# Reordered bank releases and relocated additions in the two-step q and V of layer 1

## The chip, the cores and the metric

The kernel runs on one core of one Trainium2 chip. The metric is device time in microseconds (us) of one execution. The engines are written as in the profile: PE is TensorE's matrix multiplication and PEld its weight loads, DVE is VectorE, ACT is ScalarE, POOL is GpSimd, SP is SyncE (here only a queue for transfers).

## The reference, cut to what matters

Two attention blocks over `x` of shape (8, 512, 32, 32), all in 32-bit floats: eight samples of 512 channels by 1024 positions. Layer 0 is an eight-headed attention with a group norm in front. Layer 1 has one head over all 512 channels:

```python
n = (x - mean) * rsqrt(var + EPS); n = n * gn_gamma + gn_beta      # one mean, one var per sample
q, k, v = wq @ nf + bq, wk @ nf + bk, wv @ nf + bv                 # 512 x 1024 each
attn = softmax(q.T @ k * c ** -0.5)
out = wo @ (v @ attn.T) + bo;  x = x + out
```

The kernel folds `wk` into `wq` and `wo` into `wv` before the loop, and takes the norm out of the products: `q` and `V` are made from the plain `x`, and what the norm would have added comes in as vectors (`norm.c` onto q, `norm.bias()` onto the output).

## The kernel before, in words

The loop over samples `b` runs `layer0` (64 units of layer-0 attention, then `middle`, which makes v, q and k of the next sample and projects), then `attention1` (layer 1). The order on PE, ACT and DVE is the order in which the program is written (`tc.manual_schedule(engines={PE, ACT, DVE})`); POOL and SP are ordered by the framework, close to the program. [...]

Products of 2 by 2 blocks are made in Winograd's form, seven products in place of eight (`A11·B11`, `A12·B21`, `S1·T1`, `S2·T2`, `S3·T3`, `S4·B22`, `A22·T4`, where S and T are sums of blocks). In layer 1 each of the seven is itself made in this form: the "two-step" product. q and V of samples 0 to 6 are made so by `seven_by_two_steps` (L679), called from `make_q_twice` (L1693) and `make_v_all` (L1774). It works on four groups of seven steps. Group z makes the inner products of outer products 1 and 4, w those of 5, c those of S1·T1 and A22·T4, and d those of A12·B21 and S4·B22, straight onto z. Each group has a bank of PSUM called `line` and one called `single`: `sz`/`oz`, `sw`/`ow`, `sc`/`oc`, `sd`/`od`. After each step a copy on ACT (L703) or an addition on DVE (L705) takes the bank's content to SBUF, and only then may a later step write that bank afresh. PSUM is handed out in tiles of two banks, two tiles of each tag, so c follows z in the same tiles, d follows w, and the next product's z and w follow c and d.

The first half alternates z and w, 14 steps. Then DVE makes four additions (L712 with q's bias, L710 without): `z1 += z0` for both k, `w += z1` for both k. The second half is c, c, d, c, d, c, d, ..., d, d. In its midst, after the last step of c, stand four more additions on DVE (L710): `z1 += c0` (128x512) and the long `c += w` (128x1024), for k = 1 and 0. The additions that empty the last two banks of d (`od`, `sd`) follow these in DVE's queue. After q, ACT adds the bias onto z (L736) and DVE makes `bias` (L400 to L402, three small operations). V then begins, and from step 0 on POOL makes q's sums S1 to S4 (`finish_q`, L1772, eight additions of 128x512) and the sums of S1's quarters (`halve_a`, L520, four of 128x256). After V come the scores (`line`, L1839, and `twice`, L1856), whose first banks are those of V's c and d.

The norm's averages are small matmuls (L305) into the unused second bank of z's `oz` tile (`room`, L288; `sample_average`, L302), read by DVE (L307): the mean after step 5, the variance after step 8.

`make_twice` (L583) sums the quarters of a weight for the second step and stores them in HBM; it is done once per weight. In sample 0 it runs for `v0`, `p0` and half of `wqk1` within the attention's units, on DVE, and for the other half of `wqk1` and half of `wvo1` in `middle`, on POOL, at steps 1 to 10 of v's product. Its loads and stores go through SP's queue, as does the gather of the softmax sums (`gather_couple`, L1325), on whose landing DVE's reciprocal (L1334) waits.

Of the kernel before, what the change touches and what calls it, by code (L numbers as in the profile page):

```python
# [65 lines left out]
def two_attention_blocks(  # L66
# [612 lines left out]
    def seven_by_two_steps(multiply, at, z, c, w, bias, name):  # L679

        def group(tag, products, use_of):
            line, single = (banks(t, f"ps_{t}{tag}_{name}") for t in "so")
            spares.append(single[:, 1, :])  # L690
            line, single = line[:, 0, :], single[:, 0, :]
            for bank, x, y, start, fresh, r, t in [
                (line, "A11", "B11", True, True, 0, 0), (single, "A12", "B21", True, False, 0, 0),
                (line, "S2", "T2", False, True, 0, 1), (single, "S1", "T1", True, True, 1, 1),
                (line, "S3", "T3", False, False, 1, 1), (single, "S4", "B22", False, False, 0, 1),
                (line, "A22", "T4", False, True, 1, 0),
            ]:
                multiply(bank, products, x, y, start)
                tiles, always = use_of
                to = at(tiles, r, t)  # L700
                of = bank[:, : len(products) * 2 * P].rearrange("p (i q) -> p i q", i=to.shape[1])
                if fresh and not always:
                    nc.scalar.copy(to, of)  # L703
                else:
                    nc.vector.tensor_tensor(to, of, to, ALU.add)  # L705
                yield

        def plus(to, x, y, by=None):
            if by is None:
                nc.vector.tensor_tensor(to, x, y, ALU.add)  # L710
            else:
                nc.vector.scalar_tensor_tensor(to, x, by, y, ALU.add, ALU.add)  # L712

        yield from together(group("z", REST[0], (z, False)), group("w", REST[1], (w, False)))
        for k in range(2):
            plus(z[k][:, 1, :], z[k][:, 0, :], z[k][:, 1, :], bias and bias(k, 0))
        for k in range(2):
            plus(w[k], w[k], z[k][:, 1, :], bias and bias(k, 1))
        one = group("c", [("S1", "T1"), ("A22", "T4")], (c, False))
        two = group("d", [("A12", "B21"), ("S4", "B22")], (z, True))  # L720
        spares.clear()
        next(one)
        yield
        n = 0
        for g in [one, two] * 6 + [two]:
            next(g)
            n += 1
            if n == 11:
                for k in [1, 0]:
                    plus(z[k][:, 1, :], z[k][:, 1, :], c[k][:, 0, :])  # L730
                    plus(c[k], c[k], w[k].unsqueeze(1).to_broadcast([P, 2, HALF]))
            if n < 13:
                yield
        if bias:
            for k in range(2):
                nc.scalar.activation(z[k][:, 0, :], z[k][:, 0, :], AF.Identity, bias=bias(k, 0))  # L736
        yield
        spares.clear()

# [407 lines left out]
    def layer0(bs, qs, ks, vs, b, norm_next, ending, begun):  # L1147
# [69 lines left out]
        if b == 0:  # L1217
            w = next_weight("qk13")
            w.finish()
            p0 = waiting[-1]  # L1220

            def bias0():
                rows = Rows([(bias_0, p0.moving)], 1, "bias0", room("bias0"))
                rows.store()
                rows.fetch(nc.sync)
                throughs[:] = [rows]

            hooks = {
                4: [lambda: norm_next.mean_of_all()], 5: [lambda: norm_next.variance_of_all()],
                **{6 + half: [lambda half=half: norm_next.normed(norm_next.xs, [half])] for half in range(2)},  # L1230
                8: [bias0, lambda: combine.first(norm_next.xs), lambda: score(0)],
                9: [combine.second, lambda: score(1), lambda: make_all("qk13", rows_of=both_of(w))],
            }
            hooks[7].append(p0.finish)
            at_steps(together(*pairs_qk(w, 1, bs, qs, ks, b)), hooks)
            for n, name in enumerate(["v0", "p0", "wqk1"]):
                of = [columns_of(of) for of in waiting if of.name == name]
                for i, step in enumerate(make_twice(name, rows_of=of[0] if of else None)):
                    at_units[8 + 12 * n + 2 * i - i // 3] = [step]
        else:  # L1240
            ps[0], = begun
            accs[units[0][:2]] = ps[0]
            score(1)
            if norm_next is not None:

# [249 lines left out]
    def middle(b, bs, twice_w, twice_b, comb, combine2, bias, hooks_v, divisions):  # L1495
# [3 lines left out]
        to, comb_twice, xs = {"qs": [None] * NC, "ks": [None] * NC}, {}, []  # L1499
        v_pairs = places_v(f"0_{b + 1}")  # L1500
        hooks_v.setdefault(8, []).append(lambda: twice_w.append(WeightTwice("qk02")))
        if b == 0:
            steps = [s for name in ["wqk1", "wvo1"] for s in make_twice(name, range(2, 4), None, nc.gpsimd)]
            for n, step in enumerate(steps):
                hooks_v.setdefault(1 + n, []).append(step)
        at_steps(
            make_v_twice(next_weight("v0"), twice_w.pop(0), bs, twice_b, v_pairs, f"v_0_{b + 1}"), hooks_v
        )
# [59 lines left out]
    def attention1(xs, norm, ready, b, at_values, norms):  # L1568
# [124 lines left out]
        def make_q_twice(w):  # L1693


            parts = ready.weights.all(columns_of(w))

            def multiply(bank, products, x, y, start):
                for i, (a, v) in enumerate(products):
                    nc.tensor.matmul(  # L1700
                        bank[:, i * 2 * P : (i + 1) * 2 * P], parts[a][x], twice_b[v][y],
                        start=start and i == 0, stop=True, skip_group_check=True,
                    )

            def at(tiles, r, t):
                cols = slice(t * 2 * P, (t + 1) * 2 * P)
                return tiles[r][:, :, cols] if len(tiles[r].shape) == 3 else tiles[r][:, cols].unsqueeze(1)

            z, c = ([tile2(f"{n}_q_1_{b}_{r}") for r in range(2)] for n in "zc")
            u = halves(tile2(f"w_q_1_{b}"))  # L1710

            def bias(k, i):
                return norm.c_up[:, k : k + 1] if i else norm.c[:, k : k + 1]

            of["A11"], of["A21"] = ([z[k][:, i, :] for k in range(2)] for i in range(2))
            of["A22"], of["A12"] = ([c[k][:, i, :] for k in range(2)] for i in range(2))
            return seven_by_two_steps(multiply, at, z, c, u, bias, f"q_1_{b}")

        of, hooks_v = {}, {}
        if last:  # L1720
            hooks = {
                1: [lambda: ready.measure(1), lambda: combine.make(1), lambda: combine.make(2)],
# [11 lines left out]
            (of["A11"], of["A21"]), (of["A12"], of["A22"]) = ([halves(t) for t in ts] for ts in qs)  # L1734
        else:
            hooks = {
                1: [norm.both_halves], 5: [norm.mean_of_all], 8: [norm.deviation], 12: [norm.untaken],
                16: [lambda: twice_w.append(WeightTwice("wvo1"))],
            }
            if b + 2 < B:  # L1740
# [9 lines left out]
                def measure_later(n):  # L1750
                    norms[b + 2].moments(n // 2, n % 2, n % 2 == 0)

                hooks[0], hooks[10] = ([lambda i=i: load_later(i)] for i in range(2))
                for n in range(4):
                    hooks.setdefault(15 + 3 * n, []).append(lambda n=n: measure_later(n))
                    hooks_v.setdefault(15 + 3 * n, []).append(lambda n=n: measure_later(n + 4))
                hooks_v[26] = [lambda: norms[b + 2].both_halves()]
                at_values[5] = [lambda: norms[b + 2].mean_of_all()]
                at_values[7] = [lambda: norms[b + 2].deviation()]
            at_steps(make_q_twice(w), hooks)  # L1760
        bias = norm.bias()

        w = next_weight("wvo1")

# [36 lines left out]
        if last:  # L1801
            v_pairs = places_v(f"1_{b}")
            for n in range(1, 5):
                hooks_v.setdefault(2 * n + 3, []).append(lambda n=n: finish_q(n, nc.vector))
            hooks_v[17] = [lambda: halve_a("S1")]
            at_steps(make_v_twice(w, twice_w[0], bs, twice_b, v_pairs, f"v_1_{b}"), hooks_v)
            v_of.update({(n, i): [t[:, i, :] for t in v_pairs[n]] for n in range(2) for i in range(2)})
        else:
            for n in range(1, 5):
                hooks_v.setdefault(0, []).append(lambda n=n: finish_q(n, nc.gpsimd))  # L1810
            hooks_v[0].append(lambda: halve_a("S1", None, nc.gpsimd))
            at_steps(make_v_all(w), hooks_v)


# [888 lines left out]
```

## Time and profile before

| | |
|---|---|
| three runs | 2852.02 us median (2847.18 to 2854.32) |
| the profiled execution | 2853.48 us, its span 2851.7 us |
| mean granted PE clock | 0.991 |
| PE busy | 2790.8 us, 98% of the span |
| DVE busy | 2185.8 us, 77% |
| ACT busy | 1193.4 us, 42% |
| POOL busy | 674.6 us, 24% |

The span runs from the first to the last instruction of one execution. Busy is the time in which at least one instruction of an engine runs[...]. PE's ends are modelled: a matmul of 256 columns has a record of 0.59 us for a pair while the next pair starts 0.43 us later, so a gap between products is some 0.17 us longer than the idle time that the profile writes beside it.

### The profile page before, as it was taken

How to read it: one execution, taken by the hardware profiler on the slowest of the kernel's cores; microseconds unless marked ns; L12 is line 12 of the kernel's file. 1: busy time of each engine (PE TensorE's matmuls, PEld its weight loads, DVE VectorE, ACT ScalarE, POOL GpSimd, SP SyncE). 2: the span in 40 equal slices, each digit the busy share in tenths (PEclk: the TensorE clock that was granted, in tenths of full speed). 3: DMA queues.
4: the chain of work that ended last, by engine and by line, in shares of the span. 5: the costliest groups of instructions: out<-in, count | busy, mean ns of one | idle time of the engine just before them, and what ended most of it. 6: DMA issues, size and time to landing. Idle time of an engine off the chain costs nothing. (4 is left out here: it accounts for less than half of the span.)

```text
span 2851.7 us, 42440 instructions
## 1 busy us (share of the span) xinstructions
PE 2790.8 (98%) x16570; PEld 1665.5 (58%) x16570; DVE 2185.8 (77%) x2997; ACT 1193.4 (42%) x1939; POOL 674.6 (24%) x706
## 2 busy tenths in 40 slices
PE   9998999999999999999999999999999999999999
PEld 5436674377643776437764477644776356763375
DVE  6786778876878768887778876787778877687877
ACT  3462443624346153462535524355342653226632
POOL 0003450015400254002530035300443005420021
PEclk9999999999999999999999999999999999999999
DMA  7535613255142551426423264322633236240101
GB/s 256 195 109 208 232 56 130 61 196 203 56 137 57 207 188 56 141 61 225 163 85 112 75 222 151 117 82 73 236 137 137 68 82 248 82 166 26 39 27 38
DMA packets 117552, 366.50 MB, mean 129 GB/s; under 512 B 25388, under 2 KB 26188, under 8 KB 110944
## 3 DMA queue, kind: packets, MB, share of 16 engines
q1 hardware_dynamic: 90576, 301.26, 30.7%
q10 hardware_dynamic: 26768, 62.46, 6.6%
q8 instruction: 132, 2.16, 0.3%
q14 instruction: 76, 0.62, 0.1%
HBM read 259.85 MB, written 79.99 MB: 119 GB/s over the span
## 5 line engine op out<-in xcount | busy, mean ns | idle before, releaser
L941 ACT ACTIVATE p<-s 128x1024 f32<-128x1024 f32 x505 | 516.5, 1024 | 308.5 <-PE s L1137 301.4
L943 DVE TENSOR_TENSOR acc<-acc,p 128x1024 f32<-128x1024 f32 x384 | 468.5, 1220 | 62.6 <-ACT p L941 53.9
L1137 PE MATMUL s<-qk_back,qk_back 64*64 64x512 f32 x3528 | 457.5, 590 | 0.0
L1186 PE MATMUL ps_o<-p,v_back 64*64 64x512 f32 x3528 | 455.4, 589 | 0.0
L1186 PEld LDWEIGHTS ps_o<-p,v_back 64*64 64x64 f32 x3528 | 135.0, 133 | 243.6 <-issue 240.0
L1137 PEld LDWEIGHTS s<-qk_back,qk_back 64*64 64x64 f32 x3528 | 132.6, 133 | 245.5 <-issue 216.4
L537 POOL TENSOR_TENSOR B_twice_p<-o 128x512 f32<-128x512 f32 x14 | 20.9, 1494 | 931.3 <-DVE o L1206 931.3
L2021 PE MATMUL ps_o<-t_p,s_v 128*128 128x512 f32 x384 | 169.6, 596 | 0.0
L1830 ACT ACTIVATE p<-p,factor 128x512 f32<-128x512 f32 (+1 forms) x112 | 84.6, 780 | 113.6 <-DVE p L1866 86.7
L2021 PEld LDWEIGHTS ps_o<-t_p,s_v 128*128 128x128 f32 x384 | 71.9, 190 | 88.4 <-issue 87.7
L1866 DVE TENSOR_TENSOR p<-ps_l,p 128x512 f32<-128x512 f32 x136 | 91.5, 687 | 40.3 <-PE ps_l L1856 38.3
L537 POOL TENSOR_TENSOR B_twice<-x 128x512 f32<-128x512 f32 x23 | 35.6, 1548 | 358.7 <-DVE x L1446 177.2
L1844 ACT COPY p<-ps_s 128x512 f32<-128x512 f32 x96 | 53.1, 588 | 134.4 <-PE ps_s L1839 134.4
L943 DVE TENSOR_TENSOR acc<-p,p 128x1024 f32<-128x1024 f32 x57 | 69.7, 1222 | 49.9 <-ACT p L941 49.9
L1035 PE MATMUL ps_l_qk<-t,w_qk 128*128 128x512 f32 x224 | 100.3, 595 | 0.3
L1866 DVE TENSOR_TENSOR p<-ps_s,p 128x512 f32<-128x512 f32 x112 | 74.8, 685 | 26.1 <-PE ps_s L1856 20.4
L641 ACT COPY c_q<-ps_s_qk 128x512 f32<-128x512 f32 x56 | 32.7, 583 | 140.0 <-PE ps_s_qk L1028 140.0
L1827 POOL TENSOR_TENSOR acc<-acc,p 128x512 f32<-128x512 f32 x48 | 83.6, 1741 | 13.3 <-ACT p L1830 10.8
L373 POOL TENSOR_TENSOR rstd<-rstd,minus_half 128x4 f32<-128x4 f32 (+1 forms) x16 | 12.9, 806 | 281.1 <-DVE rstd L372 281.1
L1035 PEld LDWEIGHTS ps_l_qk<-t,w_qk 128*128 128x128 f32 x224 | 42.0, 190 | 56.3 <-issue 50.2
L1839 PE MATMUL ps_s<-z_q,x 128*128 128x512 f32 x112 | 57.2, 636 | 14.1 <-DVE z_v L705 14.1
L659 DVE TENSOR_TENSOR c_v<-ps_l_v,c_v 128x512 f32<-128x512 f32 x64 | 42.6, 688 | 32.3 <-PE ps_l_v L784 32.2
(783 smaller groups left out, 6018.7 us busy)
## 6 DMA issues: line engine op xcount, KB each, us to landing
x<-in_x SPq DMA_DIRECT2D x64, 512.0 KB, 9.3
qk_back<-kept_qk SPq DMA_DIRECT2D x56, 512.0 KB, 6.3
w_qk<-stored_qk SPq DMA_DIRECT2D x14, 1792.0 KB, 8.5
fold<-acc SPq DMA_DIRECT2D x56, 256.0 KB, 3.1
qk_twice<-stored_qk_twice ACTq DMA_DIRECT2D x28, 512.0 KB, 3.9
kept_v<-c_v SPq DMA_DIRECT2D x28, 512.0 KB
kept_qk<-c_q SPq DMA_DIRECT2D x28, 512.0 KB, 3.3
kept_qk<-c_k SPq DMA_DIRECT2D x28, 512.0 KB, 3.5
```

The source lines that it names most:

```text
L537: engine.tensor_tensor(t[:, 0:4:2, :], part[:, :, 2 * P :], part[:, 0, :].rearrange("p (n q) -> p n q", n=2), ALU.subtract,)
L941: nc.scalar.activation(p, s, AF.Exp, scale=factor)
L943: nc.vector.tensor_tensor(acc, first, p, ALU.add)
L1035: nc.tensor.matmul(bank, of(i, a)[:, k, :], bs[v][:, k, :], start=start and k == 0, stop=k == 1, skip_group_check=True,)
L1137: nc.tensor.matmul(s[cols, j, :], ks[pair][k0 // HALF][rows, k0 % HALF : k0 % HALF + HD], qs[pair][g][rows, :], start=True, stop=True,)
L1186: nc.tensor.matmul(o[cols, half, :], vs[n][kt % 4 // 2][rows, h, c0 : c0 + HD], p[rows, j, :], start=kt == 0, stop=kt == NT - 1,)
L1827: engine.tensor_tensor(acc[:, i, :], acc[:, i, :], seen[i][-1], ALU.add)
L1830: nc.scalar.activation(p, p, AF.Exp, scale=norm.factor)
L1839: nc.tensor.matmul(bank, bs[v][:, k, t * P : (t + 1) * P], of[a][k], start=a == "A11" and k == 0, stop=k == 1, skip_group_check=True,)
L1844: nc.scalar.copy(to[:, t % 2, :], bank)
L1866: nc.vector.tensor_tensor(at(r, t), bank, at(r, t), ALU.add)
L2021: nc.tensor.matmul(bank, v_parts[kt // 2][a][:, kt % 2, c * P : (c + 1) * P], p_parts[kt // 2][b][:, kt % 2, cols], start=fresh and kt == ...
```

## The change

It has five parts. The first half's order becomes z, z, w, z, w, ..., w, w. In the second half, whose order stays, the additions of DVE come in another order: those that empty d's last two banks first, then `z1 += c0`; the long `c += w` go to POOL. ACT's bias onto z of q and POOL's `finish_q` and `halve_a` move from the end of q and step 0 of V to step 2 of V. `norm.bias()` and `both_halves` move into q's steps, the variance's average from step 8 to step 9, the measuring of sample b + 2 by ACT from steps 15, 18, 21, 24 to 14, 17, 19, 21. The weights' sums that POOL made in `middle` of sample 0 are made by DVE in the attention's units of sample 0, all steps from unit 3 on at a pitch of 1.5 units (before: from unit 8 on, at about 1.7 to 2).

```diff
-        yield from together(group("z", REST[0], (z, False)), group("w", REST[1], (w, False)))
+        def in_order(order, **groups):
+            for n in order:
+                next(groups[n])
+                yield
+
+        spares.clear()
+        first = dict(z=group("z", REST[0], (z, False)), w=group("w", REST[1], (w, False)))
+        yield from in_order("zzwzwzwzwzwzww", **first)
         for k in range(2):
             plus(z[k][:, 1, :], z[k][:, 0, :], z[k][:, 1, :], bias and bias(k, 0))
         for k in range(2):
             plus(w[k], w[k], z[k][:, 1, :], bias and bias(k, 1))
...
-        n = 0
-        for g in [one, two] * 6 + [two]:
-            next(g)
-            n += 1
-            if n == 11:
-                for k in [1, 0]:
-                    plus(z[k][:, 1, :], z[k][:, 1, :], c[k][:, 0, :])
-                    plus(c[k], c[k], w[k].unsqueeze(1).to_broadcast([P, 2, HALF]))
-            if n < 13:
-                yield
-        if bias:
-            for k in range(2):
-                nc.scalar.activation(z[k][:, 0, :], z[k][:, 0, :], AF.Identity, bias=bias(k, 0))
+        c_of, d_of = [("S1", "T1"), ("A22", "T4")], [("A12", "B21"), ("S4", "B22")]
+        second = dict(c=group("c", c_of, (c, False)), d=group("d", d_of, (z, True)))
+        yield from in_order("ccdcdcdcdcdcd", **second)
+        next(second["d"])
+        for k in [1, 0]:
+            plus(z[k][:, 1, :], z[k][:, 1, :], c[k][:, 0, :])
+        for k in range(2):
+            both = w[k].unsqueeze(1).to_broadcast([P, 2, HALF])
+            nc.gpsimd.tensor_tensor(c[k], c[k], both, ALU.add)
         yield
...
-            for n, name in enumerate(["v0", "p0", "wqk1"]):
+            steps = []
+            for name, ns in [("v0", range(2)), ("p0", range(2)), ("wqk1", range(4)), ("wvo1", range(2, 4))]:
                 of = [columns_of(of) for of in waiting if of.name == name]
-                for i, step in enumerate(make_twice(name, rows_of=of[0] if of else None)):
-                    at_units[8 + 12 * n + 2 * i - i // 3] = [step]
+                steps += make_twice(name, ns, of[0] if of else None)
+            for n, step in enumerate(steps):
+                at_units.setdefault(3 + 3 * n // 2, []).append(step)
...
-        if b == 0:
-            steps = [s for name in ["wqk1", "wvo1"] for s in make_twice(name, range(2, 4), None, nc.gpsimd)]
-            for n, step in enumerate(steps):
-                hooks_v.setdefault(1 + n, []).append(step)
...
+            def onto_first():
+                for k in range(2):
+                    nc.scalar.activation(z[k][:, 0, :], z[k][:, 0, :], AF.Identity, bias=bias(k, 0))
+
+            hooks_v[2] = [onto_first]
...
-                1: [norm.both_halves], 5: [norm.mean_of_all], 8: [norm.deviation], 12: [norm.untaken],
+                0: [norm.both_halves], 5: [norm.mean_of_all], 9: [norm.deviation],
+                12: [norm.untaken, lambda: biases.append(norm.bias())],
...
-                    hooks.setdefault(15 + 3 * n, []).append(lambda n=n: measure_later(n))
-                    hooks_v.setdefault(15 + 3 * n, []).append(lambda n=n: measure_later(n + 4))
+                    hooks.setdefault([14, 17, 19, 21][n], []).append(lambda n=n: measure_later(n))
+                    hooks_v.setdefault([14, 17, 19, 21][n], []).append(lambda n=n: measure_later(n + 4))
...
-        bias = norm.bias()
+        bias = biases[0] if biases else norm.bias()
...
-                hooks_v.setdefault(0, []).append(lambda n=n: finish_q(n, nc.gpsimd))
-            hooks_v[0].append(lambda: halve_a("S1", None, nc.gpsimd))
+                hooks_v[2].append(lambda n=n: finish_q(n, nc.gpsimd))
+            hooks_v[2].append(lambda: halve_a("S1", None, nc.gpsimd))
```

The last sample makes q and V by other functions (`make_q`, `make_v_twice`) and is not touched.

More of the change, by code (lines that the diff above doesn't have):

```diff
@@ L718, in seven_by_two_steps @@
             plus(w[k], w[k], z[k][:, 1, :], bias and bias(k, 1))
-        one = group("c", [("S1", "T1"), ("A22", "T4")], (c, False))
-        two = group("d", [("A12", "B21"), ("S4", "B22")], (z, True))
         spares.clear()
-        next(one)
-        yield
-        n = 0
-        for g in [one, two] * 6 + [two]:
-            next(g)
-            n += 1
-            if n == 11:
-                for k in [1, 0]:
-                    plus(z[k][:, 1, :], z[k][:, 1, :], c[k][:, 0, :])
-                    plus(c[k], c[k], w[k].unsqueeze(1).to_broadcast([P, 2, HALF]))
-            if n < 13:
-                yield
-        if bias:
-            for k in range(2):
-                nc.scalar.activation(z[k][:, 0, :], z[k][:, 0, :], AF.Identity, bias=bias(k, 0))
+        c_of, d_of = [("S1", "T1"), ("A22", "T4")], [("A12", "B21"), ("S4", "B22")]
[7 more added lines that the diff above has]
+            nc.gpsimd.tensor_tensor(c[k], c[k], both, ALU.add)
         yield
@@ L1717, in make_q_twice @@
             return seven_by_two_steps(multiply, at, z, c, u, bias, f"q_1_{b}")
-        of, hooks_v = {}, {}
+        of, hooks_v, biases = {}, {}, []
         if last:
@@ L1751, in measure_later @@
                     norms[b + 2].moments(n // 2, n % 2, n % 2 == 0)
-                hooks[0], hooks[10] = ([lambda i=i: load_later(i)] for i in range(2))
+                for i in range(2):
+                    hooks.setdefault(10 * i, []).append(lambda i=i: load_later(i))
                 for n in range(4):
-                    hooks.setdefault(15 + 3 * n, []).append(lambda n=n: measure_later(n))
-                    hooks_v.setdefault(15 + 3 * n, []).append(lambda n=n: measure_later(n + 4))
+                    hooks.setdefault([14, 17, 19, 21][n], []).append(lambda n=n: measure_later(n))
+                    hooks_v.setdefault([14, 17, 19, 21][n], []).append(lambda n=n: measure_later(n + 4))
                 hooks_v[26] = [lambda: norms[b + 2].both_halves()]
```

## The prediction

> **What bounds the kernel now.** I read the page first, then the granted clock, then PE's waits.
>
> ```profile
> span 2851.7 us, 42440 instructions
> PE 2790.8 (98%) x16570; PEld 1665.5 (58%) x16570; DVE 2185.8 (77%) x2997; ACT 1193.4 (42%) x1939; POOL 674.6 (24%) x706
> ```
> ```profile
> core 0: 2851.7 us, clock 0.991
> ```
> ```profile
> PE ps_sw_v L1782 <- DVE z_q L705: 21.7, 7, 3.1
> PE ps_s L1839 <- DVE z_v L705: 14.1, 7, 2.0
> PE ps_l_v L784 <- DVE c_v L659: 9.4, 1, 9.4
> PE ps_oz_q L1700 <- DVE mean_m L307: 1.8, 7, 0.3
> ```
>
> PE sets the end. It idles 2851.7 - 2790.8 = 61 us, and 0.009 of the clock costs another 26 us, so no reordering can win more than 87. Three waits for DVE hold 45 of the 61: the start of V (seven times), the start of the scores (seven times), and one long wait in sample 0. A table by stage, one stretch per sample from q's first product to the end of the scores' first block, says what these stages lose together (columns: stretch, us, then each engine's busy time, clock, DMA):
>
> ```profile
> 1719.73:1795.17 75.44, 69.34 (x359) 55.97 (x358) 47.77 (x76) 32.16 (x72) 34.14 (x48) 0.93 0.35 129
> 2071.02:2143.88 72.86, 65.76 (x359) 52.32 (x358) 50.29 (x76) 31.96 (x72) 35.55 (x48) 1.00 0.37 134
> sum 515.86, PE 472.14 PEld 380.53 DVE 343.60 ACT 212.32 POOL 240.97; mean PE 67.45 PEld 54.36 DVE 49.09 ACT 30.33 POOL 34.42
> ```
>
> The products alone, at the distance at which they follow each other undisturbed in the timeline (q 0.86 us, w's half as much; V 0.89 and 0.445; scores 1.72 and 0.86), need 21.1 (q) + 21.8 (V) + 19.8 (scores) + 0.3 (averages) = 63.0 us. Seven samples take 515.9, so 515.9 - 441 = **75 us** is lost. The timeline of sample 3 shows the cause: the long addition stands before the two that empty banks.
>
> ```profile
> 1394.77 1.22 DVE L710 TENSOR_TENSOR c_q<-c_q,w_q 128x1024 f32<-128x1024 f32 x1
> 1395.92 0.68 DVE L705 TENSOR_TENSOR z_q<-ps_od_q,z_q 128x512 f32<-128x512 f32 x1
> 1396.52 0.68 DVE L705 TENSOR_TENSOR z_q<-ps_sd_q,z_q 128x512 f32<-128x512 f32 x1
> 1397.25 0.71 PE L1782 MATMUL ps_sw_v<-w_wvo,t 128*128 128x128 f32 x4 [3.10 <-DVE z_q L705]
> ```
>
> [...] from 1397 to 1402 us the granted clock averages 0.66, and V's 128-column products follow at twice their distance. Laid on the trace's clock events, a window with 2.16 us of idle or more was followed by a slow one, one with 2.13 or less was not; each slow window costs 1.7 us of work. [...] in sample 5, where DVE's middle additions of V met POOL's 128x256 sums:
>
> ```profile
> 2108.34 1.85 POOL L520 TENSOR_TENSOR S_twice<-s_q 128x256 f32<-128x256 f32 x2
> 2108.76 1.98 DVE L710 TENSOR_TENSOR z_v<-z_v 128x512 f32<-128x512 f32 x2 [0.93 <-ACT z_v L703]
> 2110.67 2.35 DVE L710 TENSOR_TENSOR w_v<-w_v,z_v 128x512 f32<-128x512 f32 x2
> 2113.67 0.60 PE L1782 MATMUL ps_oc_v<-wvo_twice,T_twice 128*128 128x128 f32 x3 [0.16 <-DVE c_v L705]
> ```
>
> Undisturbed two of these take 1.28. Here they alternate strictly with POOL, 1.14 us for each pair, which is 0.68 + 0.73 less 0.27 of overlap. [...]
>
> **The change, part by part** (per sample of the seven; V starts at 0).
>
> *1. Banks first, end of q.* d's last addition now runs 0.2 to 0.9, and w's first step, third in the new order, wants the bank at 2 x 0.89 = 1.8. The 3.1 wait goes. *End of V:* the same; the second score line wants its bank at 1.72 + 0.86 = 2.6, free at 0.9. The 2.0 wait goes. The waits for ACT's copy of z7 (0.4 each, q and V) go too, as two steps of w now follow z7. ACT's moved bias (2 x 0.72) lies before the copy of z3, wanted three steps later: nothing. The measuring keeps its place in ACT's queue relative to the copies: nothing.
>
> *2. Long additions on POOL.* By the slope of POOL's rows (0.73 for 256 columns, 1.27 for 512) one of 1024 takes 2.4. They start when `z1 += c0` is done (2.2): 2.2 to 7.0. q's sums queue behind them: 8 x 1.23, to 16.9; S1's quarters, 4 x 0.68, to 19.6 (before: at 16.6 of V). The scores need those more than 26 us after V's start: hidden. But DVE's four middle additions of V come at 9.4, and POOL is now in its 128x512 sums until 17. A pair costs 0.68 + 1.27 - 0.27 = 1.68. First wait some 0.6, then 0.55 + 3 x 1.68: done at 15.6, c2's addition behind them at 16.3 to 16.4. The fourth step of c (its bank is c2's) is due at 9.3 + 5 x 0.89 = 13.8. **A new stall of 2.7** (1.9 to 3.1 by the first wait; 0.2 if DVE were let through). With 2.7 us, the chance that 2.16 of it lie in one window is (3.41 - 2.16 + 0.54) / 3.41 = 0.52, so 0.9 us of clock.
>
> *3. Long additions after V.* On POOL they meet DVE's sums of A12's quarters (four of 128x256) in the scores: DVE waits for two of 2.4, then alternates with S4's. The addition behind them ends near 9.1 after the scores begin, wanted at 9.5: nothing, bounds 0 and 2. POOL's later sums stand some 9 us later relative to PE than before; their first user comes 12 us after this block: nothing.
>
> *4. Averages.* The row `ps_oz_q <- mean_m` shows that the two banks of a tile are one to the waits. The mean now follows z4, which wrote that tile and must be copied first: 0.2 + 0.58 + 0.06 = 0.84. The variance follows z6 and its DVE addition: 0.2 + 0.69 + 0.06 = 0.95. Before, the wait lay behind the average: 0.42 and 0.46. *`norm.bias()` in q:* three small operations, 0.5, and the order's end put q's middle additions 1.3 to 1.7 later; c4 of q then waits 0.5 (0 to 0.9). Before, those three took 0.85, 1.2 and 1.18, blocked by POOL.
>
> Losses after: 0.84 + 0.95 + 0.5 + 2.7 + 0.9 = 5.9 per sample, 41 in seven, against 75. **Gain 34.**
>
> *5. Weights' sums of sample 0.* SP held the gather behind two stores that waited for POOL, DVE's reciprocal behind the gather, PE behind DVE:
>
> ```profile
> 245.09 2.08 SPq L611 DMA_DIRECT2D stored_wvo_twice<-wvo_twice  x2
> 247.27 0.59 SPq L1330 DMA_DIRECT2D few<-sums  x1
> 249.52 0.35 DVE L1334 RECIPROCAL few<-few 128x32 f32<-128x32 f32 x1 [10.53 <-DMA few<-sums]
> 251.06 1.22 PE L784 MATMUL ps_l_v<-w_v,t 128*128 128x256 f32 x2 [9.35 <-DVE c_v L659]
> ```
>
> 9.5 of stall go, and three slow windows (10.2 us at half clock), 5.1: 14.6. The other samples show no such wait, so none comes next. In the attention DVE gets six more sums of 4 x 0.24 us, 5.7, and five more loads, which land 3.1 to 4.5 us after issue where the first sum comes 1.8 to 3.6 later. DVE was idle 10.6 of the 80 us from 120 to 200, PE never: I take 1 us of cost, bounds 0 and 6. **Gain 13.6.**
>
> The sum: 2851.7 - 34 - 13.6 = 2804. The profiled execution was 1.8 longer than its span and 1.5 over the median: **2805**. A measurement of this kernel tells some 0.3% (8.6 us) from no change.
>
> **The rivals.** *B, DVE is let through* (or POOL's sums run elsewhere): part 2's stall and its clock vanish, 7 x 3.4 = 24: 2781. The strict alternation in sample 5 speaks against it; POOL's order is not the program's, which speaks for some of it. *C, the lock costs more*: the scores' addition is late by 2 each sample, the new V stall always trips the clock (0.8 more), the attention costs 6: 2805 + 20 + 5 = 2830. Part 3's margin of 0.4 us speaks for it. *D, slower*: a broadcast 128x1024 addition on POOL is far from linear. Beyond 2.6 us each, every us more in the two delays the scores' addition by two. At 6 us PE waits 6.8 there in each sample and loses two windows (3.4), with 1 of POOL's lateness elsewhere: 7 x 11 = 78: 2883. It ends slower from 4.9 us on (4.6 + 1.7 of clock, 7 x 6.3 = 44, and C's attention). POOL's rows at two widths lie on a line through 0.2, which speaks against it. *E*: the averages trip no clock, 0.84 and 0.95 being 2.6 us apart.
>
> **How the numbers follow.** A (the sum above) 0.62, its own range 2794 to 2818; B 0.18; C 0.13; D 0.05, a mishap that nothing shows 0.02. The range 2782 to 2831 takes in the ends of the unknown costs and most of B and C. Faster by over 0.3%: 0.91; within: 0.04; slower: 0.05.
>
> **What would show it.** Right: no rows `ps_sw_v <- z_q`, `ps_s <- z_v`, `ps_l_v <- c_v`; new rows of PE for `ps_oc_v <- DVE c_v` near 2.5 each and L305 behind `z_q` of ACT and DVE, 0.7 and 0.8 each; DVE's middle additions of V near 1.7 each; the seven stretches near 69 us. Wrong: a wait over 3 us in the scores, in V's first half or in the first attention; POOL's long additions over 3 us.

## The result, and the profile after

The changed kernel takes **2815.39 us** (median of 4 runs, 2814.06 to 2822.12) against 2852.23 for the kernel before (4 runs): a ratio of **0.9878, 95% interval 0.9858 to 0.9899**. The forecast was 2805 (2782 to 2831). The medians differ by 36.8 us, where 47 was forecast. The profiled execution took 2814.56 us, with a span of 2812.1, 39.6 less than before. The first lines of the page after, and the granted clock:

```profile
span 2812.1 us, 42413 instructions
PE 2771.6 (99%) x16570; PEld 1648.4 (59%) x16570; DVE 2197.6 (78%) x2993; ACT 1197.3 (43%) x1939; POOL 741.0 (26%) x710
```
```profile
core 0: 2812.1 us, clock 0.999
```

PE does the same 16570 matmuls in 19 us less busy time, as the clock rose from 0.991 to 0.999, and idles 41 us where it idled 61. PE's waits after (engine, tile, line, releaser; then us in total, times, longest):

```profile
PE ps_oc_v L1786 <- DVE c_v L705: 18.9, 7, 2.7
PE ps_oz_q L305 <- DVE z_q L705: 6.1, 7, 0.9
PE ps_oz_q L305 <- ACT z_q L703: 5.4, 7, 0.8
PE ps_sum L1315 <- DVE acc L1307: 2.3, 1, 2.3
```

The three waits that held 45 us are gone, each as forecast. Four new ones took their place. The first, at V's fourth step of c, is the new stall of the prediction's step 2 (2.7 there, 2.7 here). The next two are step 4's averages. The last, in the first attention, the prediction only had as part of a bound. The seven stretches from q's start to the end of the scores' first block say how evenly it goes (stretch, us, busy PE, PEld, DVE, ACT, POOL, granted clock, DMA share, GB/s):

```profile
1351.49:1420.45 68.96, 64.50 (x359) 52.06 (x358) 50.11 (x72) 32.56 (x72) 42.77 (x49) 1.00 0.39 141
2040.46:2110.80 70.34, 65.87 (x360) 53.42 (x358) 50.06 (x72) 32.56 (x72) 42.85 (x49) 0.98 0.38 139
sum 484.19, PE 452.91 PEld 365.81 DVE 350.84 ACT 216.39 POOL 297.95; mean PE 64.70 PEld 52.26 DVE 50.12 ACT 30.91 POOL 42.56
```

They took 515.86 before and 484.19 now: 31.7 us of the 39.6. Sample 5 alone met a slow window (3.41 us in which PE is granted half its clock) and is 1.4 longer. The rest of the gain, 7.6 us, is there when q of sample 0 starts (325.66 us before, 318.03 after).

The new stall in the timeline of V, sample 3 (start, us, engine, line, operation; V starts at 1375.68, lines of one engine are merged where they follow each other):

```profile
1384.92 2.95 POOL L1776 TENSOR_TENSOR s_q<-s_q,z_q 128x512 f32<-128x512 f32 x2
1385.15 3.27 DVE L710 TENSOR_TENSOR z_v<-z_v 128x512 f32<-128x512 f32 x2
...
1387.84 3.39 POOL L1776 TENSOR_TENSOR s_q<-z_q 128x512 f32<-128x512 f32 x2
1388.34 3.43 DVE L710 TENSOR_TENSOR w_v<-w_v,z_v 128x512 f32<-128x512 f32 x2
1391.70 0.68 DVE L705 TENSOR_TENSOR c_v<-ps_oc_v,c_v 128x512 f32<-128x512 f32 x1
1392.43 1.16 PE L1786 MATMUL ps_oc_v<-wvo_twice,T_twice 128*128 128x128 f32 x8 [2.70 <-DVE c_v L705]
```

DVE's four middle additions need 6.6 us, 1.65 each (1.68 forecast, 0.64 undisturbed), one for each of POOL's sums beside them (1.70 for each of the two at 1387.84, 1.27 for the one at 1383.69). The addition that empties the bank stands behind them, and PE behind that. Which of POOL's works made this, and what each part of the change is worth, is what the experiments ask.

### The profile page after: what moved, and what is told of

It reads as the page before. It is cut to its first block, busy times and chain, and to the rows that moved or that the text cites. A ratio compares the mean times of both kernels' runs of the same rounds, so it can differ in the third digit from the quotient of the medians.

```text
span 2812.1 us, 42413 instructions
## 1 busy us (share of the span) xinstructions
PE 2771.6 (99%) x16570; PEld 1648.4 (59%) x16570; DVE 2197.6 (78%) x2993; ACT 1197.3 (43%) x1939; POOL 741.0 (26%) x710
## 3 DMA queue, kind: packets, MB, share of 16 engines
q8 instruction: 132, 2.16, 0.3%
## 4 chain that ended last, share of the span: by engine, by line
PE 93%; DVE 3%; issue 2%; DMA 1%; ACT 0%; ACTq 0%; SPq 0%; POOL 0%; DVEq 0%; POOLq 0%
PE ps_o L1185 15%; PE s L1136 14%; PE ps_o L2025 10%; PE ps_l L1860 5%; PE ps_l_qk L1034 5%; PE ps_s L1843 4%; PE ps_s L1860 4%; PE ps_s_qk L1027 3%; PE ps_l_v L783 3%; PE ps_l_p L768 3%; PE ps_o_qk L1027 2%; PE ps_s_v L1055 2%; PE ps_s_p L1092 2%; PE ps_s_two L2155 2%; PE ps_o_v L1055 2%
## 5 line engine op out<-in xcount | busy, mean ns | idle before, releaser
L661 DVE SCALAR_TENSOR_TENSOR c_q<-ps_l_qk,vec,c_q 128x512 f32<-128x512 f32 x56 | 40.8, 749 | 34.2 <-PE ps_l_qk L1034 33.8
L659 DVE TENSOR_TENSOR c_v<-ps_l_v,c_v 128x512 f32<-128x512 f32 x64 | 42.7, 689 | 31.3 <-PE ps_l_v L783 31.2
```

## The experiments

The theory: PE's new stall comes from POOL's sums of q meeting DVE's middle additions, and the gain comes from DVE being free at V's start. The rivals: the order of the additions alone pays; POOL's long additions cause the stall; the new order of z and w frees the banks. No run takes part 3 (POOL's sums and ACT's bias from step 2 on) or the early `norm.bias()` by itself. Each ratio below is to the kernel before on the same chip, with its 95% interval.

### POOL's sums held back (e1_gate)

```diff
-            for n in range(1, 5):
-                hooks_v[2].append(lambda n=n: finish_q(n, nc.gpsimd))
-            hooks_v[2].append(lambda: halve_a("S1", None, nc.gpsimd))
+            hooks_v[2].append(lambda: finish_q(1, nc.gpsimd))
+            for n in range(2, 5):
+                hooks_v.setdefault(14, []).append(lambda n=n: finish_q(n, nc.gpsimd))
+            hooks_v[14].append(lambda: halve_a("S1", None, nc.gpsimd))
...
             of[f"S{n}"] = halves(tile2(f"s{n}_q_{b}"))
+            if n == 2 and u_of:
+                part = of["S2"][0][:, :NC]
+                engine.tensor_tensor(part, u_of[1][:, :NC], u_of[1][:, :NC], ALU.add)
...
             u = halves(tile2(f"w_v_1_{b}"))
+            u_of.extend(u)
```

> In V of samples 0 to 6, POOL's sums S2 to S4 of q now wait until DVE's four middle additions are done (a 4-column POOL instruction ahead of S2 reads what the last of them wrote). Theory, POOL's 128x512 sums and DVE's middle additions exclude each other: each middle addition takes 0.65 to 0.7 us in place of 1.63 to 1.75, PE's wait for c_v falls from 2.7 to 0.2 us in each sample, the one slow clock window of sample 5 goes too: 7 x 2.5 + 1.4 = 19 less, about 2796 us. Rival, the additions are late for another reason (ACT's copies, or a wait shifted to the scores, whose sums S now come up to 3 us later): the wait stays at 2.7 or as much comes back in the scores, 2815 us.

**2791.06 us, ratio 0.9792 (0.9778 to 0.9805)**, 24.3 less than the changed kernel. The wait for `c_v` is not in the list any more. The timeline of V's middle in sample 3 of this kernel:

```profile
1374.61 2.19 DVE L710 TENSOR_TENSOR z_v<-z_v 128x512 f32<-128x512 f32 x2
1376.73 1.28 DVE L710 TENSOR_TENSOR w_v<-w_v,z_v 128x512 f32<-128x512 f32 x2
1377.93 0.68 DVE L705 TENSOR_TENSOR c_v<-ps_oc_v,c_v 128x512 f32<-128x512 f32 x1
1378.09 0.20 POOL L1773 TENSOR_TENSOR s_q<-w_v 128x4 f32<-128x4 f32 x1 [2.43 <-DVE w_v L710]
```

DVE waits once for the sum that POOL is still in (2.19 for two), then runs free (1.28 for two), and POOL's next sum starts behind it. V's second half falls from 15.52 to 12.55 us. So the stall was these sums, and nothing came back in the scores (19.78 us against 19.89). It is the prediction's rival B made by hand, priced there at 24 less. More was gained than the 19 expected of the run: a wait of 2.7 cost 2.97 of PE's time (15.52 less 12.55), and the slow window in the first attention did not fall here (q of sample 0 starts 1.3 earlier).

### The long additions on DVE (e3_dvelong), and the order alone (e11_order)

```diff
-            nc.gpsimd.tensor_tensor(c[k], c[k], both, ALU.add)
+            nc.vector.tensor_tensor(c[k], c[k], both, ALU.add)
```

> The long additions c += w (128x1024) run on DVE behind the two additions z1 += c0, not on POOL, nothing else. Theory, their move to POOL pays by leaving DVE free at V's start: DVE is 2.5 us later there, the bank oz of V is freed at 5.4 us in place of 2.9 and PE waits 1.5 to 2.0 in V's first half; POOL starts q's sums 2.2 us earlier, so the middle additions meet fewer of them and the wait for c_v falls from 2.7 to 1.5 or 2.5; in the scores nothing: 7 x (+0.8 to +1.5), about 2823 us (2815 to 2832). Rival, POOL's long additions are what pushes its sums into the middle additions, and without them the wait for c_v is gone: below 2808 us.

**2836.92 us, ratio 0.9950 (0.9936 to 0.9963)**: 21.5 slower than the changed kernel, against 8 expected. PE's waits in it:

```profile
PE ps_oc_v L1786 <- DVE c_v L705: 12.9, 7, 1.9
PE ps_oz_v L1786 <- DVE z_v L705: 11.2, 7, 1.6
PE ps_s L1860 <- DVE p L1870: 11.2, 7, 1.6
```

The first two are as expected. The third was not: with the long additions of V on DVE, the addition in the scores comes 1.6 late. There the prediction's step 3 had given POOL's version a margin of 0.4 us, and DVE's has none. Three more slow windows in V (four, where the changed kernel has one) took some 5 us of the 21.5. The rival falls as the whole cause: without the long additions on POOL the middle additions still wait, though the stall is 1.9 where it was 2.7.

The other half of the question, in the kernel before:

```diff
-            if n == 11:
+            if n == 13:
```

> The kernel before with one number changed: the four additions of DVE in the second half (z1 += c0, c += w) come after the two that empty d's last banks, all still on DVE; no other part of the change. From e3_dvelong (2836.9 with the long additions on DVE, against 2839.0 for part 5 alone): the order alone only shifts PE's waits, V's start (3.1) and the scores' start (2.0) go, and in their place come the bank oz of V (about 1.6), the scores' addition onto p (1.6) and c_v in V's middle (1.9): 2850 us, within 8. Rival, the order is the part that pays, as the prediction's step 1 has it (3.1 + 2.0 a sample and fewer slow windows): 2820 us or less.

**2860.70 us, ratio 1.0029 (1.0017 to 1.0040)**: the order alone makes the kernel slower, by 0.3%. The two waits that it aims at go, and these come:

```profile
PE ps_oz_v L1782 <- DVE z_v L705: 32.9, 7, 5.0
PE ps_s L1856 <- DVE p L1866: 11.2, 7, 1.6
```

The wait for `oz` is three times what I expected, and the timeline of sample 3 says why (V starts at 1400.03):

```profile
1403.61 2.17 DVE L710 TENSOR_TENSOR c_q<-c_q,w_q 128x1024 f32<-128x1024 f32 x1
1405.71 0.15 DVE L400 TENSOR_TENSOR both<-mean_m,rstd 128x1 f32<-128x1 f32 x1
1405.86 1.26 POOL L1772 TENSOR_TENSOR s_q<-z_q,c_q 128x512 f32<-128x512 f32 x1 [1.16 <-DVE both L400]
1405.89 1.26 DVE L401 TENSOR_SCALAR bias<-v_g,both 128x4 f32<-128x4 f32 x1
...
1407.18 1.18 DVE L402 TENSOR_TENSOR bias<-v_b,bias 128x4 f32<-128x4 f32 x1
1408.28 0.68 DVE L705 TENSOR_TENSOR z_v<-ps_oz_v,z_v 128x512 f32<-128x512 f32 x1
1409.02 1.22 PE L1782 MATMUL ps_oz_v<-wvo_twice,B_twice 128*128 128x128 f32 x4 [4.65 <-DVE z_v L705]
```

The second long addition takes 2.17 in place of 1.22, and two operations on four columns, 0.23 and 0.16 us long in the changed kernel, take 1.26 and 1.18: POOL has begun its sums. All of it now stands ahead of the addition that frees `oz`. So it takes the order together with what leaves DVE's queue at V's start: the long additions, as e3_dvelong shows, and by this timeline `norm.bias()`, which no run moves alone. The order alone loses, and without the long additions' move most of the gain is gone: the seven stretches of e3_dvelong take 508.7 us, only 7 of the 31.7 less than before.

### The order of z and w (e8_zw)

```diff
-        yield from in_order("zzwzwzwzwzwzww", **first)
+        yield from in_order("zwzwzwzwzwzwzw", **first)
...
-                0: [norm.both_halves], 5: [norm.mean_of_all], 9: [norm.deviation],
+                0: [norm.both_halves], 5: [norm.mean_of_all], 8: [norm.deviation],
```

> The changed kernel with the first half's order of before (z, w, z, w, ...) and the averages after steps 5 and 8 as before; DVE's order, POOL's additions and the rest stay. Theory, the order of DVE's additions frees the banks and not the order of z and w: per sample q's first half is 0.8 us shorter (the averages wait less), V's first half 0.6 longer (0.3 for the bank sd at w's first step, 0.35 for ACT's copy of z7): about 2814 us. Rival, z, z, w is what takes PE off the bank that is emptied last: PE waits over 1.5 us at V's start, 2826 us or more.

**2813.63 us, ratio 0.9868 (0.9849 to 0.9887)**, the same as the changed kernel. q's first half is 0.77 shorter (10.86 us), V's first half 0.55 longer (9.93), which leaves 2.1 of the 2.7 us at c_v; four samples met slow windows in place of one. So the new order of z and w is not what pays. What it spares in waits for ACT's copy of z7 and for V's bank, it gives back at the averages and in a longer stall at c_v: a stretch without a slow window takes 68.2 to 68.5 us here and 69.0 in the changed kernel. The three more slow windows, 1.6 each, hide that.

### The averages in another bank (e4_ow)

```diff
-        ps = room(name, 0)
+        ps = room(name, in_w[0])
...
-                0: [norm.both_halves], 5: [norm.mean_of_all], 9: [norm.deviation],
+                0: [norm.both_halves], 5: [lambda: beside_w(norm.mean_of_all)], 9: [lambda: beside_w(norm.deviation)],
...
+        def beside_w(average):
+            in_w[0] = 1
+            average()
+            in_w[0] = 0
```

> The norm's two averages in q of samples 0 to 6 are written to the spare second bank of w's tile in place of z's, at the same steps, nothing else. Theory, an average waits for the copy or addition that empties the tile's other bank, and w's was emptied earlier: both waits (0.8 and 0.9 us shown, with the pipeline gap 1.0 and 1.1) go, 7 x 2.0 = 14 less, about 2801 us. Rival, the averages wait for their input from POOL or for the order on PE: 2815 us.

**2813.75 us, ratio 0.9868 (0.9849 to 0.9887)**: no gain in sum, though both waits are gone and q's first half falls from 11.63 to 9.57 us in every sample, the 2.06 expected. Two things took it back. q's second half starts 2 us earlier, and ACT's measuring, which stands ahead of copies of c in ACT's queue, now waits for its load; the seven second halves of q are 5.7 us longer in sum. From the timeline of sample 3:

```profile
1365.29 0.63 ACT L335 ACTIVATE mean<-x_stat 128x512 f32<-128x512 f32 x1 [2.41 <-DMA x_stat<-in_x]
1368.64 1.13 PE L1699 MATMUL ps_sc_q<-T_twice,wqk_twice 128*128 128x256 f32 x4 [0.82 <-ACT c_q L705]
```

And V, shifted in time, now meets the clock's windows otherwise, which takes 8.3 us more. V's second half in samples 0 and 1 of this kernel (columns as in the stretches above):

```profile
351.14:366.65 15.51, 12.82 (x115) 12.63 (x114) 12.75 (x14) 8.56 (x21) 13.13 (x17) 1.00 0.00 1
693.78:710.92 17.14, 14.45 (x114) 14.25 (x113) 12.76 (x14) 8.56 (x21) 13.13 (x17) 0.90 0.00 1
```

The same work with the same stall of 2.7 us: 15.51 us at full clock, 17.14 at 0.90. Six of seven samples run so here, one of seven in the changed kernel. The price of this stall was its length, plus 1.6 (17.14 less 15.51 here) or 1.4 (16.88 less 15.52 in sample 5 of the changed kernel) where a slow window followed it.

### The weights' sums (e7_sums, e2_pitch2, e5_pause)

e7_sums is the kernel before with the two hunks of part 5 alone:

```diff
-            for n, name in enumerate(["v0", "p0", "wqk1"]):
+            for name, ns in [("v0", range(2)), ("p0", range(2)), ("wqk1", range(4)), ("wvo1", range(2, 4))]:
...
+                at_units.setdefault(3 + 3 * n // 2, []).append(step)
...
-            steps = [s for name in ["wqk1", "wvo1"] for s in make_twice(name, range(2, 4), None, nc.gpsimd)]
-            for n, step in enumerate(steps):
-                hooks_v.setdefault(1 + n, []).append(step)
```

> The kernel before with part 5 alone (the weights' sums of sample 0 all made by DVE in the attention, as in the changed kernel). By the trace of the changed kernel PE is 4.7 us later at the end of the attention and 7.6 us earlier at q of sample 0: 2850 - 7.6 = about 2843 us (2838 to 2848, as later stalls may meet other clock windows). By the prediction's step 5, 13.6 less: 2837 us. Rival, part 5 gives nothing by itself: 2850 us.

**2839.01 us, ratio 0.9957 (0.9942 to 0.9972)**: 11.7 less. q of sample 0 starts at 315.93 us, 9.7 earlier than before. In the stretches, whose waits are those of before, 4.8 us went with the clock windows (511.1 us against 515.9). So part 5 gives 8 to 10 and not 13.6.

A fold is DVE's addition of the two halves of a softmax sum (L1307), which come together by three transfers in SP's queue (`fold<-acc` twice, `acc<-acc`). There are four in a sample. What the expectations call the first fold is the second of them, at 177.5 us in the changed kernel, on which PE's first sums (L1315) wait.

Two attempts to remove the cost of part 5, the wait of 2.3 at that fold:

```diff
-                at_units.setdefault(3 + 3 * n // 2, []).append(step)
+                at_units.setdefault(3 + 2 * n, []).append(step)
```

> The weights' sums of sample 0 come at every second unit of the attention in place of every 1.5 units, nothing else. Theory, DVE's queue is too full at the first fold of the softmax sums: PE's wait of 2.3 us at L1315 and the slow clock window behind it (together 4.6 us of lateness) go, about 2811 us. Rival, the wait comes from the landing of the weight loads or from the fold's transfers and not from DVE's backlog, or it shows at the next fold: 2815 us.

**2817.28 us, ratio 0.9887 (0.9871 to 0.9902)**, no gain. The wait at L1315 fell to 1.4, and 2.0 came at the end of the attention (`ps_o_v` for DVE's `o`). What is left of the wait is the expectation's rival, the landing of a load. DVE stood idle for it just ahead of the fold, which follows at 176.60:

```profile
174.53 0.29 DVE L520 TENSOR_TENSOR wqk_twice<-again_wqk 128x128 f32<-128x128 f32 x1 [2.69 <-DMA again_wqk<-stored_wqk]
```

```diff
-                at_units.setdefault(3 + 3 * n // 2, []).append(step)
+                unit = 3 + 3 * n // 2
+                at_units.setdefault(unit + 7 * (unit > 34), []).append(step)
```

> The changed kernel with one edit: the weights' sums of sample 0 keep their pitch of 1.5 units, but those due from unit 35 on come 7 units later, so that none stands in DVE's queue in the units ahead of the first fold of the softmax sums. Theory, DVE's backlog makes that fold late: PE's wait of 2.3 us at L1315 and the slow clock window behind it go, 4.6 us in the span up to q of sample 0, about 2811 us if later stalls meet no more slow windows than now. Rival, the fold's own transfers in SP's queue are late: the wait stays at 1.4 us or more, 2815 us.

**2827.40 us, ratio 0.9919 (0.9904 to 0.9934)**, worse by 12. In the profiled execution 7.0 of it are there when q of sample 0 starts, and two more slow windows in V take 3.2. PE's new wait, and an idle time of DVE ahead of it:

```profile
PE ps_o_v L1055 <- DVE o L1192: 5.1, 1, 5.1
```
```profile
212.10 0.29 DVE L520 TENSOR_TENSOR wvo_twice<-again_wvo 128x128 f32<-128x128 f32 x1 [5.01 <-DMA again_wvo<-stored_wvo]
```

The wait at L1315 fell to 1.3, by the one sum taken from in front of the fold (four operations of 0.28 us, started 0.2 to 0.3 apart), and 5.1 came at the attention's end. That is not DVE's work alone. DVE waits 5.0 us for a load, issued at 205.88 behind a fold's transfers in SP's queue, and from there to the late `o` at 232.36 it has no idle time in which to catch up.

### What beats both (e6_best, e9_nopause, e10_early)

e6_best joins e1_gate, e5_pause and e4_ow, with the measuring in q two steps later and the bias out of the way:

```diff
-                12: [norm.untaken, lambda: biases.append(norm.bias())],
+                12: [norm.untaken], 22: [lambda: biases.append(norm.bias())],
...
-                    hooks.setdefault([14, 17, 19, 21][n], []).append(lambda n=n: measure_later(n))
+                    hooks.setdefault([16, 18, 20, 22][n], []).append(lambda n=n: measure_later(n))
```

> All that paid put together: the gate of e1_gate, the pause of e5_pause, the averages in w's spare bank as in e4_ow, and, since that brings q's second half 2 us closer to the landing of x_stat, the measuring in q at steps 16, 18, 20, 22 in place of 14, 17, 19, 21, and norm.bias() at step 22 in place of 12. Expected from the e1_gate run: averages 7 x 2.06 = 14.4, the wait for c_q in q 7 x 0.3 = 2, the first fold 4.6: 2791 - 21 = 2770 us. Rival, ACT's queue waits for x_stat again and holds the copies of c: 2775 to 2780 us.

**2783.50 us, ratio 0.9764 (0.9748 to 0.9780)**. The stretches were 63.4 to 64.3 us; the pause cost its 7 at the attention's end again (q of sample 0 at 323.58 us), and again DVE waited for loads there, 3.6 and 6.1 us. e9_nopause against e6_best:

```diff
-                unit = 3 + 3 * n // 2
-                at_units.setdefault(unit + 7 * (unit > 34), []).append(step)
+                at_units.setdefault(3 + 3 * n // 2, []).append(step)
...
-                    hooks.setdefault([16, 18, 20, 22][n], []).append(lambda n=n: measure_later(n))
+                    hooks.setdefault([17, 20, 22, 24][n], []).append(lambda n=n: measure_later(n))
```

> As e6_best without the pause in the weights' sums (3 + 3n//2 for all, as in the changed kernel), and with the measuring in q at steps 17, 20, 22, 24. Theory, the pause only moved DVE's backlog to the end of the attention, where it cost 7 us (e5_pause: q of sample 0 starts at 325.0 us, 318.0 without); the averages and the gate add up: e1_gate's 2791 less 7 x 2.06 for the averages less 7 x 0.3 for the first wait in q's second half: 2775 us. Rival, the loss at the end of the attention comes from something else in e6_best: 2783 us as there.

**2772.70 us, ratio 0.9725 (0.9708 to 0.9742)**, 42.7 less than the changed kernel. Its clock is 1.000. Its stretches summed:

```profile
sum 444.27, PE 444.27 PEld 365.56 DVE 312.26 ACT 215.73 POOL 285.92; mean PE 63.47 PEld 52.22 DVE 44.61 ACT 30.82 POOL 40.85
```

PE is busy in all of it: 444.27 us, where the prediction put the products alone at 7 x 63.0 = 441. PE waits for nothing that the profile shows in these stages, so order has little left to win there.

e10_early against e9_nopause (`begin` is the step that issues a group's loads):

```diff
-            for n, step in enumerate(steps):
+            at_step = list(range(len(steps)))
+            begins = [n for n in at_step if steps[n].__name__ == "begin"]
+            for early, n in zip(begins[3:], begins[4:]):
+                at_step[n] = early
+            for n, step in sorted(zip(at_step, steps), key=lambda x: x[0]):
```

> As e9_nopause, with the weights' loads for the sums of wqk1 and wvo1 issued one group (4.5 units) earlier; the sums stand at the same units. Theory, 1.0 of PE's wait of 2.3 us at the first fold is DVE waiting for such a load to land (again_wqk, 1.0 us at 169 us in the changed kernel): the wait falls to about 1.2 and the window behind it is no longer slow: 1 to 3 us less than e9_nopause. Rival, DVE is full without it and the fold is as late: the same as e9_nopause.

**2773.39 us, ratio 0.9730 (0.9713 to 0.9747)**, the same. DVE no longer waits for a load, yet the wait at L1315 is 2.8, against 1.6 without the edit. The run does not settle its question, because it lengthened another wait of DVE, at the fold before:

```profile
152.66 1.23 DVE L1313 TENSOR_TENSOR acc<-acc,fold 128x1024 f32<-128x1024 f32 x1 [5.10 <-DMA acc<-acc]
```

In e9_nopause this wait is 2.27. The early loads now stand ahead of that fold's transfers in SP's queue, and the last of the transfers is issued at 148.83 where it was at 147.16. So the edit took away a wait of 0.47 for a load and made one for the fold's transfers 2.8 longer.

## Why the prediction was right, and where it was off

The sign was right, and so were the places of the waits that went and of those that came. Of the 47 us forecast, 36.8 came between the medians (39.6 of 47.7 from span to span). By its own steps:

- **Step 1** (the waits at V's and the scores' start go): they went, all fourteen. That this is the reordering's work alone is not so: e11_order makes the same reordering and is 0.3% slower. The steps priced the parts in the change's company, where they hold.
- **Step 2** (a new stall of 2.7): 2.7 in each sample, from POOL's sums beside DVE's middle additions, as e1_gate shows. A long addition took 2.35 to 2.75 us on POOL, with medians of 2.55 and 2.53 (2.4 estimated); rivals B (DVE let through) and D (far from linear) fall with this. In the changed kernel's timeline DVE's middle additions, with both inputs in SBUF, and POOL's 128x512 sums take turns (the "lock" of rival C): 1.65 us for a pair, where the addition takes 0.64 and the sum 1.27 undisturbed. DVE's 335 additions of 128x512 with an input in PSUM that overlap work of POOL there take 0.67 to 0.69 us, the 460 others 0.63 to 0.69. The clock's part was off: 0.9 a sample forecast, 0.2 measured. The chance of 0.52, an estimate from the limit of 2.16 us and the slow windows of 3.41 us in the trace of the kernel before, meant three or four slow windows in the seven samples, and one fell; with the same stall six fell in e4_ow, three each in e2_pitch2 and e5_pause. So some 4 us of the gain were luck, by that estimate.
- **Step 3** (no cost in the scores): right, by a hair. The addition ended 9.4 us after the scores began (9.1 forecast, wanted at 9.5), and the block took 19.89 us against 19.78 with no stall at all.
- **Step 4**: the averages cost 2.06 where 0.84 + 0.95 stood, by e4_ow. The waits themselves, 0.8 and 0.9, were right; the pipeline's gap behind each, some 0.17, was left out. c4 of q cost 0.4 where 0.5 stood: q's second half is 12.56 us, 12.17 in e9_nopause.
- **Together**, losses of 5.9 a sample were forecast over 63.0, and 6.2 measured (484.2 / 7 - 63.0): gain 31.7 against 34. The 63.0 was 0.44 too low, as a stretch without stalls takes 63.44 in e9_nopause. The other 5.7 are 2.97 for the stall, 2.06 for the averages, 0.4 for c4, 0.2 for the clock and 0.1 in the scores. The averages and the clock miss in opposite directions.
- **Step 5** is the term that was off by most: 7.6 against 13.6. Its cost in the attention was put at 1 with bounds 0 and 6, and was 4.7. DVE's idle share (10.6 us of 80 in the kernel before) was read as room, but the sums arrive in a queue that has to be empty by the fold at 177.5 us. From the timeline of the changed kernel:

```profile
172.81 3.88 DVE L942 TENSOR_TENSOR acc<-acc,p 128x1024 f32<-128x1024 f32 x3
176.61 0.28 DVE L520 TENSOR_TENSOR wqk_twice<-again_wqk 128x128 f32<-128x128 f32 x1
...
177.54 1.22 DVE L1307 TENSOR_TENSOR acc<-acc,fold 128x1024 f32<-128x1024 f32 x1
178.82 1.17 PE L1315 MATMUL ps_sum<-acc,ones 64*32 64x512 f32 x8 [2.31 <-DVE acc L1307]
```

Three of the attention's additions in a row show the backlog, then a weights' sum, then the fold, 3.1 us later than before (174.47). The sums' own time is not all of it. From the fold before this one on, DVE is idle twice, both times for a transfer, and never for want of work:

```profile
150.43 1.22 DVE L1307 TENSOR_TENSOR acc<-acc,fold 128x1024 f32<-128x1024 f32 x1 [2.34 <-DMA acc<-acc]
169.21 0.29 DVE L520 TENSOR_TENSOR wqk_twice<-again_wqk 128x128 f32<-128x128 f32 x1 [1.00 <-DMA again_wqk<-stored_wqk]
```

In the kernel before it waits for neither. In the changed kernel SP's queue waits for a weights' sum that it is to store, and the first two transfers of the fold at 150.43 stand behind that store (141.12, then 141.48 and 142.05). From SP's waits, 118 to 150 us:

```profile
SPq L611 <- DVE p_twice L520: 7.7, 1, 7.7
```

It is the pattern that the prediction found in `middle`, a transfer behind a store that waits for a sum, made anew in the attention. The prediction had listed the loads' landing too, and priced all of it at 1. No run has the sums without these two waits, so how the 4.7 divides between the sums' own time and the waits (3.3 in sum) is not shown.

Its gain was also too high, 14.6 against 12.3. The three slow windows of the kernel before:

```profile
244.34:247.75 3.41, 0.00 (x0) 0.00 (x0) 0.00 (x0) 0.00 (x0) 2.33 (x6) 0.50 0.39 160
247.75:251.17 3.42, 0.11 (x1) 0.11 (x1) 1.65 (x4) 0.00 (x0) 0.00 (x0) 0.50 0.25 80
251.17:254.58 3.41, 3.41 (x8) 2.75 (x9) 0.44 (x1) 0.32 (x2) 0.00 (x0) 0.50 0.56 157
```

The prediction counted half of all three, 5.1 us, on top of the stall. But PE worked in the third alone (0.00, 0.11 and 3.41 us busy), so the clock cost 1.7; the first two lie inside the stall of 9.5. In all, 12.3 less the stall leaves 2.8. e7_sums gives the same 12.3: PE is 2.6 later at the end of the attention and 9.7 earlier at q of sample 0.

The wait at L1315 is 1.6 in e7_sums and e9_nopause and 2.3 in the changed kernel, with the same sums at the same units. Most of the difference is the wait for the load at 169 us, 1.00 in the changed kernel and 0.46 and 0.47 in the other two. Why that load lands later stays open.

## What to carry to other kernels

Putting the additions that free a bank first lost 0.3% alone (e11_order) and was part of a gain of 1.2% where what stood behind them had left the queue before the next bank fell due: list the whole queue to that point, small operations too, at the durations they have beside GpSimd (1.26 us in e11_order for one of 0.23 in the changed kernel). Work moved to GpSimd came back here as lateness of DVE where DVE's additions read both inputs from SBUF (1.65 us each, 0.64 undisturbed); hold it until DVE's critical additions are through, with a data dependence if need be. DVE's idle share was no room for a job ahead of a deadline (4.7 us of cost, where 1 was taken): look for the transfers that the job brings as well. A load that DVE's queue waited for (5.0 us in e5_pause), and a store in SP's queue that held up a fold's transfers (DVE waited 2.34 us for them in the changed kernel), delayed what stood behind.

## What the runs showed of the hardware

The same stall had two prices: V's second half with its stall took 15.52 us in sample 3 of the changed kernel and 16.88 in sample 5, 15.51 and 17.14 in two samples of e4_ow (granted clock 1.00 and 0.90 in both pairs). Where it lay in time decided. In the clock records of all 13 traces the slow stretches (granted clock 0.5) begin on one grid of 3.413 us, the windows of the prediction. Counting PE's idle time in each window by the profile's records, every window at full clock with 2.0 us or more of it (60, ten of them in the kernel before with 2.02 to 2.99) was followed by a slow one, and none below 1.8 was; between the two it went either way. In the changed kernel the stall of sample 5 put 2.17 us into one window, and the other six at most 1.91. In e4_ow six put in 2.26 to 2.70, and the one that passed 1.74. The prediction's limits of 2.13 and 2.16 come out of the kernel before with the pipeline's gap added (1.96 and 2.02 by the records), but the lower one holds for windows at full clock alone. A window that was itself slow was followed by another from 0.63 us of idle on (13 cases, among them 0.74 and 0.63 in the kernel before), and up to 0.54 never (52 cases).

So edits that shifted the start by a few us changed how many samples paid, and with it the total, by some 8 us between e4_ow (six slow windows in V) and the changed kernel (one). Executions of one kernel differed too: the changed kernel's four ran from 2814.06 us at a mean clock of 0.999 to 2822.12 at 0.996. Without stalls five of the seven stretches of e9_nopause took 63.44 us each, the other two 63.51 and 63.56.
